# Two-layer graph kernel in fp32: when the scores are masked, squared, scaled and turned, and when the weights' factors are formed

## The chip, the cores and the metric

The kernel runs on one core of one Trainium2 chip. The metric is the device time of the slowest core, here the only one, in microseconds (us), as the median of several runs.

## The reference

64 graphs of 256 nodes and 512 features share one 0/1 adjacency matrix. Two layers are added to the stream x, each behind a layer norm and a relu. What is computed, cut to its core:

```python
h = relu(layernorm(x))                       # layer 0
q, k, v = h @ Wq.T, h @ Wk.T, h @ Wv.T
rel = adj.T * (q @ k.T)                      # scores, masked
rel = rel / norm(rel, axis=2)                # each row to length 1
x = x + rel @ v
h = relu(layernorm(x))                       # layer 1
x = x + (adj @ h) @ weight + bias
```

## The kernel before

The 64 graphs go in 32 pairs. Everything is fp32 and lives in SBUF. Wq and Wk are multiplied once into one matrix M, so that for a pair the work on TensorE is a chain of products: G (h times M), V (h times Wv), the scores (h times G), attend (scores times V, added to x), the gather (adjacency times the second h, called y), and the mix (y times the weight, added to x).

The large products are done by Winograd's form of Strassen's algorithm: seven products of half-size blocks instead of eight. `winograd_steps` (L184) calls them by number, in the order 1, 5, 6, 3, 7, 2, 4, in three PSUM banks: 1, 6, 7 and 4 accumulate one after the other in bank_a. After each product its `take` reads the bank: ScalarE (ACT) copies where the target is new, else VectorE (DVE) adds. `two_levels` (L209) does the same for G, V and the mix, with a second level for two of the products: its steps are called a1, c5, a6, c (a second reading of bank_c), a7, a4, and g1 to g4 (the second-level parts, in bank_d and bank_e). The next product in a bank waits until the last reader of the bank has ended.

The seven products need sums of blocks as operands, and these are DVE work in lists of "steps": `right_operands` (L128, instructions L135 to L138) and `left_factors` (L166, L173 to L176), four instructions each. By use: `gs` for G, `sums` for the transposed h of a later pair, `h_second` and `y_second` for second levels, `y_steps` for the gathered y, `v_steps` and `rel_steps` for the operands of attend (from V and from the turned scores), `w_steps` and `wv_steps` for the weights; `w_second_steps`, `wv_second_steps` and `m_second_steps` for the second level of the weights, once each in the first pairs.

Around the scores (`scores`, L542) there are, for a pair: two masks on DVE (L561, one for each half k of the columns), four squares with row sums on ACT (L566), a root on ACT (L572), an inverse on DVE (L575), four scales on ACT (L578), `place` (L580: 16 transfers on SyncE's queue, which move 32x32 blocks into `placed`), and four 32x32 block transposes on DVE, `turns` (L588, `placed` to `turned`). `turned_i` and `sums_i` (L450, L173 to L176) are the like for the h of pair i; `relus` (L342), `uppers` (L703, ACT) and `lowers` (L707, DVE) form the second h and its split into two parts for exact products at a reduced format; `add_bias` (L719) is four adds on GpSimd (POOL), each possible once ACT has read its quarter of x (the relu).

The order is written out by hand. `run_steps` (L277) calls product after product, and after product n the steps in slot n of a dictionary; TensorE, DVE and ACT keep exactly that order, each in its own queue. In a steady pair (`steady`, L997) the order on TensorE is: attend of pair i interleaved with the rest of V (`attend_and_v`), the scores of pair i+1, G and part of V of pair i+2 (`g_and_v`, L907), the gather of pair i, and the mix of pair i with two parts of G and V (`mix_and_v`, L916). 28 pairs are steady; `first_pairs` (L926) and `last_pairs` (L1045) write out the rest.

The parts of attend by number are `one`, `five`, `six`, `three`, `two`, `seven`, `four` (L672); the mix's g4 follows `one`. `six` reads the operand which `rel_steps[2]` (L175) forms. `norm_by_scalar` (L348) works out the first norm of pair i+4 in the mix: totals and squares on ACT, its root and end.

Of the kernel before, what the change touches and what calls it, by code (L numbers as in the profile page):

```python
# [19 lines left out]
def kernel(  # L20
# [137 lines left out]
    def run(steps):  # L158
        for step in steps:
            step()  # L160
# [112 lines left out]
    def winograd(product, take, side={}, early=False):  # L273

        run_steps(winograd_steps(product, take, early), side)
# [263 lines left out]
        products = v_products(i)  # L539
        return two_levels(*products, *second_weights_moving(HL2[i], wv_second, V[i]))  # L540

    def scores(i, side={}, by_matmul=False):  # L542


        left, right = HL.pop(i), G.pop(i)
        rel = work.tile([P, NB, NC, N], F32, tag="rel", name=f"rel_{i}")
        placed = work.tile([P, NB, NC, NC, P], F32, tag="placed", name=f"placed_{i}")
        turned = work.tile([P, NB, NC, NC, P], F32, tag="turned", name=f"turned_{i}")
        rn = small.tile([P, NB, NC], F32, tag="rn", name="rn")
        R[i] = turned, rel, placed  # L550
# [25 lines left out]

        def scale(b, k):
            nc.scalar.activation(rel[:, b, k], rel[:, b, k], AF.Copy, scale=rn[:, b, k : k + 1])  # L578

        def place():  # L580
            rv = rel.rearrange("p b k (t m) -> p (b k t) m", m=P)
            pv = placed.rearrange("p b k t n -> p (b k t) n")
            for j in range(P // S):
                for k in range(P // S):
                    nc.sync.dma_start(out=pv[ts(j, S), :, ts(k, S)], in_=rv[ts(k, S), :, ts(j, S)])

        def turn(b, k):
            nc.vector.transpose(turned[:, b, :, k], placed[:, b, k])  # L588

        def each(f):  # L590
            return [(lambda b=b, k=k: f(b, k)) for k in range(NC) for b in range(NB)]

        def turn_at_once():
            for b in range(NB):
                pt = ps_m.tile([P, T], F32, tag="pm", name="pr")
                for t in range(NC):
                    for k in range(NC):
                        nc.tensor.transpose(
                            pt[:, ts(t * NC + k, P)], rel[:, b, k, ts(t, P)], ident
                        )  # L600
                nc.scalar.copy(turned[:, b].rearrange("p t k n -> p (t k n)"), pt)

        winograd(product_of_tokens(left, right), take, side)
        if by_matmul:
            masks = [lambda: mask(0), lambda: mask(1)]
            return masks, each(square_sum), root, inverse, rn, turn_at_once
        return (
            [lambda: mask(0), lambda: mask(1)], each(square_sum), root, inverse, each(scale), place,
            each(turn),
        )  # L610

# [102 lines left out]
    def add_bias(i):  # L714

        xt = flat(X[i])
        add = nc.gpsimd.tensor_tensor
        return [
            (lambda c=c: add(xt[:, c, :], xt[:, c, :], bias_bc, ALU.add)) for c in range(TC)  # L719
        ]  # L720
# [205 lines left out]
    def first_pairs(exact):  # L926
# [13 lines left out]
        gs = g_operands(0)  # L940
# [18 lines left out]
        turned2, sums2 = transpose_blocks(2)  # L959
        project_v(1, {  # L960
            0: gs[0:2], 1: gs[2:3] + turned2[0:2], 2: gs[3:4] + turned2[2:4] + relus[0:2],
            3: turned2[4:6] + relus[2:4], 4: turned2[6:8] + m_second_steps[0:4],
            5: m_second_steps[4:8] + turns[0:2], 6: turns[2:4],
        })
        place_blocks(3)
        masks, squares, norm_root, inverse, scales, place, turns = scores(1, {
            0: sums2[0:1], 1: sums2[1:2], 2: sums2[2:3], 3: sums2[3:4], 5: wv_second_steps[0:4],
            6: wv_second_steps[4:8],
        })
        stats, *parts = ln1(0, exact)  # L970
        h_second = second_h.pop(2)()
# [4 lines left out]
        if exact:  # L976
            nc.vector.tensor_copy(adjt_r, adjt_sb)
        g, v = g_and_v(2, by_slot(layer_1(parts), {
            1: h_second + [inverse], 3: scales + [place], 4: turned3[0:1] + add_bias(0), 5: turned3[1:3],
            6: turned3[3:4],  # L980
        }))
        v_steps, rel_steps = attend_operands(1)
        y_steps = gather(0, exact, {
            0: turned3[4:6], 1: turned3[6:8], 2: sums3[0:1], 3: sums3[1:2] + w_second_steps[0:4],
        })
        y_second = second_of_y(0)
        totals, mean, row_squares, *norm0 = norm_by_scalar(flat(X[4]))
        run(y_steps[0:2])
        mixed = mix_and_v(0, g, v, {
            0: y_steps[2:4] + totals[0:2], 1: y_second[0:4] + totals[2:4],  # L990
            2: w_second_steps[4:8] + y_second[4:8] + [mean] + row_squares[0:2],
            3: v_steps[0:2] + row_squares[2:4], 4: turns + rel_steps[0:2] + norm0[0:2],
            5: v_steps[2:4] + sums3[2:4],
        })
        return norm0[2], rel_steps[2:4], mixed, v

    def steady(i, exact, relu0, rel_steps, mixed, v):  # L997

# [5 lines left out]
        stats, root, end, relus, uppers, lowers = ln1(i, exact)  # L1004
        halves = [stats[b * NC + t] for t in range(NC) for b in range(NB)]
        attend_and_v(i, mixed, v, {
            0: rel_steps + relus0[0:2], 1: relus0[2:4] + gs[0:1], 2: gs[1:2],
            3: gs[2:3], 4: gs[3:4] + halves[0:1], 5: halves[1:2],
        })
        if i + 4 < NP:  # L1010
# [3 lines left out]
        h_second = second_h.pop(i + 2)()  # L1014
        masks, squares, norm_root, inverse, scales, place, turns = scores(i + 1, {
            0: halves[2:3], 1: halves[3:4] + h_second[0:1], 2: [root] + h_second[1:4],
            3: [end] + relus[0:1], 4: relus[1:2], 5: uppers[0:1], 6: uppers[1:2],
        })
        turned, sums = transpose_blocks(i + 3)
        bias_steps = add_bias(i)  # L1020
        v_steps, rel_steps = attend_operands(i + 1)
        g, v = g_and_v(i + 2, {
            0: masks + squares[0:2] + lowers[0:1],
            1: squares[2:4] + [norm_root] + lowers[1:2] + turned + [inverse],
            2: relus[2:4],
            3: scales + [place] + sums[0:2],
            4: uppers[2:4] + lowers[2:3] + sums[2:4] + bias_steps,
            5: lowers[3:4] + v_steps[0:2],
        })
        y_products, y_steps = gather_steps(i, exact)  # L1030
        run_steps(y_products, {2: y_steps[0:1]})
        y_second = second_of_y(i)
        totals, row_squares, mean, ends, relu0 = [], [], [], [], None
        if i + 4 < NP:
            totals, step, row_squares, root0, end0, relu0 = norm_by_scalar(flat(X[i + 4]))
            mean, ends = [step], [root0, end0]
        run(y_steps[1:2])
        mixed = mix_and_v(i, g, v, {
            0: y_steps[2:4] + totals[0:2], 1: y_second[0:4] + totals[2:4],
            2: y_second[4:8] + mean + row_squares[0:2],  # L1040
            3: turns + row_squares[2:4], 4: rel_steps[0:2] + ends, 5: v_steps[2:4],
        })
        return relu0, rel_steps[2:4], mixed, v

    def last_pairs(exact, relu0, rel_steps, mixed, v):  # L1045
# [5 lines left out]
        attend_and_v(a, mixed, v, {  # L1051
            0: rel_steps, 1: gs[0:1], 2: gs[1:2], 3: gs[2:3], 4: gs[3:4] + halves[0:1],
            5: halves[1:2],
        })
        h_second = second_h.pop(c)()
        masks, squares, norm_root, inverse, scales, place, turns = scores(b, {
            0: halves[2:3], 1: halves[3:4] + h_second[0:1], 2: [root] + h_second[1:4],
            3: [end] + relus[0:1], 4: relus[1:2], 5: uppers[0:1], 6: uppers[1:2],
        })
        g, v = g_and_v(c, {  # L1060
            0: masks + squares[0:2] + lowers[0:1],
            1: squares[2:4] + [norm_root] + lowers[1:2],
            2: relus[2:4] + [inverse],
            3: scales + [place],
            4: uppers[2:4] + lowers[2:3] + add_bias(a),
            5: lowers[3:4],
        })
        y_steps = gather(a, exact)
# [89 lines left out]
```

## Time and profile before

The median of 3 runs is 1742.64 us (1741.23 to 1745.06). The profiled execution has a span of 1740.6 us at a granted clock of 0.999. One middle pair, from the start of its scores to the start of the next, by stage:

| stage (us from the span's start) | length | PE busy | DVE busy | ACT busy | POOL busy |
|---|---|---|---|---|---|
| scores 887.24 to 893.67 | 6.43 | 6.43 | 5.60 | 2.64 | 0.45 |
| G and V 893.67 to 908.36 | 14.69 | 14.69 | 13.64 | 10.94 | 5.01 |
| gather 908.36 to 912.08 | 3.72 | 3.72 | 2.55 | 1.76 | 0.00 |
| mix 912.08 to 925.57 | 13.49 | 13.49 | 11.59 | 7.21 | 0.00 |
| attend 925.57 to 940.12 | 14.55 | 13.76 | 14.05 | 3.52 | 0.77 |
| sum | 52.88 | 52.09 | 47.43 | 26.07 | 6.22 |

PE is the time in which matmuls are under way, and a matmul held up inside such a stretch doesn't show as idle. A row of a timeline has the start in us, the length in us, the engine, the line, the operation, and output<-inputs; in brackets the idle time of the engine before it and what ended that. Rows of one kind that follow each other are merged (x4). A row of the waits has the total, the number and the longest, in us.

### The profile page before, as it was taken

What the parts mean: (1) busy time and instruction counts of PE and PEld (TensorE: products, weight loads), DVE (VectorE), ACT (ScalarE), POOL (GpSimd) and SP (SyncE); (2) the same over time, 40 slices, a digit from 0 to 9 for tenths busy, and PEclk for the clock granted to TensorE, in tenths of its full rate; (3) what the DMA queues carried; (4) which work ended last, traced back from release to release, by engine and by line L of the source; (5) the groups of instructions that cost most, each with busy time, mean ns of one, the idle gap of its engine ahead of it and who ended that gap; (6) DMA issues with size and microseconds to landing.
All of it is one profiled execution on the core that took longest, in us unless ns stands there. A gap on an engine that the chain in (4) does not pass through costs nothing.

```text
span 1740.6 us, 28453 instructions
## 1 busy us (share of the span) xinstructions
PE 1698.9 (98%) x10274; PEld 1531.7 (88%) x10274; DVE 1523.9 (88%) x3336; ACT 818.3 (47%) x1835; POOL 198.2 (11%) x167
## 2 busy tenths in 40 slices
PE   9999999999999999999999999999999999999997
PEld 7978888898888988888988889988889888889976
DVE  7788989889898889898889898898988898988776
ACT  3444444544445554445544455444455544453331
POOL 0011100111101111001111011110011110011111
PEclk9999999999999999999999999999999999999999
DMA  7413342243332343331343422433323433223101
GB/s 240 63 25 85 75 85 61 38 85 81 78 78 49 57 86 77 82 74 35 74 84 75 86 52 46 85 80 79 79 45 59 86 76 84 69 30 61 34 28 51
DMA packets 425734, 122.56 MB, mean 70 GB/s; under 512 B 398064, under 2 KB 398832, under 8 KB 425584
## 3 DMA queue, kind: packets, MB, share of 16 engines
q1 hardware_dynamic: 412992, 80.28, 25.5%
q0 software_dynamic: 8432, 32.51, 5.3%
q10 hardware_dynamic: 4160, 7.87, 1.3%
q8 instruction: 83, 1.36, 0.3%
q14 instruction: 67, 0.55, 0.1%
HBM read 38.27 MB, written 33.55 MB: 41 GB/s over the span
## 4 chain that ended last, share of the span: by engine, by line
PE 84%; DVE 14%; issue 1%; ACT 0%; DMA 0%; ACTq 0%; DVEq 0%
PE bank_a L299 22%; PE bank_a L287 13%; PE bank_a L311 7%; PE py L735 6%; PE bank_c L299 6%; PE bank_a L658 5%; PE bank_e L525 4%; PE bank_c L287 3%; PE bank_e L478 3%; PE bank_d L525 3%; PE bank_c L311 3%; PE bank_d L478 2%; DVE x_ring L534 2%; PE bank_b L311 2%; DVE x_ring L769 1%; PE bank_b L658 1%
## 5 line engine op out<-in xcount | busy, mean ns | idle before, releaser
L719 POOL TENSOR_TENSOR x_ring<-x_ring,bias_bc 128x512 f32<-128x512 f32 x128 | 173.2, 1374 | 736.5 <-DVE rel L558 443.8
L299 PE MATMUL bank_a<-wv_t,ht 128*128 128x256 f32 x768 | 181.7, 379 | 0.0
L287 PE MATMUL bank_a<-ht,m_t 128*128 128x256 f32 x768 | 181.4, 379 | 0.0
L513 ACT COPY v<-bank_a 128x512 f32<-128x512 f32 x96 | 55.6, 580 | 253.4 <-PE bank_a L299 253.4
L287 PEld LDWEIGHTS bank_a<-ht,m_t 128*128 128x128 f32 x768 | 145.9, 190 | 19.8
L299 PEld LDWEIGHTS bank_a<-wv_t,ht 128*128 128x128 f32 x768 | 143.5, 190 | 18.3
L364 ACT ACTIVATE blocks<-x_ring,sm 128x512 f32<-128x512 f32 x112 | 80.9, 722 | 125.0 <-DVE sm L361 123.2
L735 PE MATMUL py<-adjt_r,h 128*128 128x256 f32 x1024 | 125.9, 280 | 0.1
L342 ACT ACTIVATE h2c<-x_ring,nb,rs 128x512 f32<-128x512 f32 x128 | 97.4, 807 | 56.8 <-DVE nb L339 50.1
L299 PE MATMUL bank_a<-w_t,ys 128*128 128x256 f32 x512 | 121.4, 380 | 0.3 <-DVE x_ring L769 0.3
L735 PEld LDWEIGHTS py<-adjt_r,h 128*128 128x128 f32 x1024 | 120.0, 188 | 0.3 <-DVE h L707 0.3
L790 POOL DMA_DIRECT2D out_dram<-x_ring x31 | 24.1, 776 | 784.9 <-issue 568.1
L739 ACT COPY yt<-py 128x512 f32<-128x512 f32 x128 | 75.0, 587 | 73.2 <-PE py L735 53.8
L299 PEld LDWEIGHTS bank_a<-w_t,ys 128*128 128x128 f32 x512 | 94.9, 190 | 16.0 <-DVE x_ring L769 0.9
L377 ACT ACTIVATE h<-x_ring,nb,rs 128x512 f32<-128x512 f32 x112 | 82.0, 803 | 53.8 <-PE bank_e L525 53.8
L769 DVE TENSOR_TENSOR x_ring<-bank_a,x_ring 128x512 f32<-128x512 f32 x128 | 86.9, 679 | 21.7 <-PE bank_a L299 21.5
L561 DVE TENSOR_TENSOR rel<-rel,adjt_sb 128x512 f32<-128x512 f32 x64 | 68.4, 1106 | 41.3 <-ACT rel L556 41.3
L311 PE MATMUL bank_a<-ht,gt 128*128 128x128 f32 x744 | 101.3, 279 | 0.4 <-DVE rel L558 0.4
L330 DVE BATCH_NORM_STATS2 st<-x_ring 128x6 f32<-128x512 f32 x144 | 97.8, 679 | 0.4
L556 ACT COPY rel<-bank_a 128x256 f32<-128x256 f32 x96 | 35.4, 369 | 129.5 <-PE bank_a L311 58.9
L311 PEld LDWEIGHTS bank_a<-ht,gt 128*128 128x128 f32 x744 | 90.4, 192 | 3.6 <-DVE rel L558 0.6
L665 DVE TENSOR_TENSOR x_ring<-bank_a,x_ring 128x512 f32<-128x512 f32 x116 | 78.8, 679 | 10.7 <-PE bank_a L658 10.7
(221 smaller groups left out, 4084.7 us busy)
## 6 DMA issues: line engine op xcount, KB each, us to landing
blocks<-h SPq DMA_DIRECT2D x496, 64.0 KB, 3.6
out_dram<-x_ring POOLq DMA_DIRECT2D x31, 1024.0 KB, 5.4
x_ring<-in_x_dram SPq DMA_DIRECT2D x28, 1024.0 KB, 6.1
placed<-rel SPq DMA_DIRECT2D x496, 32.0 KB, 2.0
x_ring<-in_x_dram ACTq DMA_DIRECT2D x4, 1024.0 KB, 5.4
wq_sb<-in_L_gnn_Wq_dram SPq DMA_DIRECT2D x4, 256.0 KB, 4.7
wk_sb<-in_L_gnn_Wk_dram ACTq DMA_DIRECT2D x4, 256.0 KB, 6.0
wv_sb<-in_L_gnn_Wv_dram ACTq DMA_DIRECT2D x1, 1024.0 KB, 5.5
```

The source lines that it names most:

```text
L287: nc.tensor.matmul(bank[:, e * HT_ : (e + 1) * HT_], right[n][:, d, ts(e, P)], left[n][:, d, :], start=(start and e == 0 and d == 0), stop ...
L299: nc.tensor.matmul(bank[:, b * HD : (b + 1) * HD], left[n][:, d, ts(b, P)], right[n][:, d, :], start=(start and b == 0 and d == 0), stop=( ...
L311: nc.tensor.matmul(bank[:, ts(b, P)], right[n][:, d, ts(b, P)], left[n][:, d, ts(b, P)], start=(start and b == 0 and d == 0), stop=(d == H ...
L330: nc.vector.bn_stats(st[:, c, :], src[:, c, :])
L342: nc.scalar.activation(dst, src[:, c, :], AF.Relu, bias=nb[:, c : c + 1], scale=rs[:, c : c + 1])
L377: nc.scalar.activation(dst, src[:, c, :], AF.Relu, bias=nb[:, c : c + 1], scale=rs[:, c : c + 1])
L478: nc.tensor.matmul(out, m_second[k][n], HL2[i][k][n], start=start, stop=True, skip_group_check=True)
L525: nc.tensor.matmul(out, left[k][n], right[k][n], start=start, stop=True, skip_group_check=True)
L658: nc.tensor.matmul(bank[:, ts(b, HD)], left[n][:, b], right[n][:, b], start=(start and b == 0), stop=True, skip_group_check=True,)
L719: (lambda c=c: add(xt[:, c, :], xt[:, c, :], bias_bc, ALU.add)) for c in range(TC)
L735: nc.tensor.matmul(pm[:, d, :], left[:, b * NC + m, ts(d0 + d, P)], right, start=(n == 0), stop=(n == len(terms) - 1),)
L769: nc.vector.tensor_add(xt[block], bank.rearrange("p (b e) -> p b e", b=NB), xt[block])
```

## The change

Four things move; no instruction on TensorE is added, removed or reordered.

- In `scores` with `inside=True`, the mask and the squares of the half k = 1 of the columns, which is complete after the fifth product, go into slots 5 and 6 of the scores. The other half, the root, the inverse, the scales and `place` go into slot 0 of G, ahead of the uppers, which leave the scores.
- `turns` go from slot 3 of the mix to the end of the gather, ahead of `y_steps[1]`.
- All four `rel_steps` then run in slots 3 and 4 of the mix; before, the last two ran in slot 0 of attend.
- In the first pairs the second-level factors of the weights, and the transposes and sums of pair 3, are dealt out differently; in the last mix but one `y_second[4:8]` comes a slot earlier, and the lowers a slot later.

What it is for: operands of attend are to be ready before attend begins.

```diff
-    def scores(i, side={}, by_matmul=False):
+    def scores(i, side={}, by_matmul=False, inside=False):
...
+        masks, squares = [lambda: mask(0), lambda: mask(1)], each(square_sum)
+        if inside:
+            side = by_slot(side, {5: masks[1:], 6: squares[2:]})
+            masks, squares = masks[:1], squares[:2]
         winograd(product_of_tokens(left, right), take, side)
...
     # first_pairs
         project_v(1, {
-            3: turned2[4:6] + relus[2:4], 4: turned2[6:8] + m_second_steps[0:4],
+            3: turned2[4:6] + relus[2:4] + w_second_steps[0:4],
+            4: turned2[6:8] + m_second_steps[0:4],
...
         masks, squares, norm_root, inverse, scales, place, turns = scores(1, {
-            0: sums2[0:1], 1: sums2[1:2], 2: sums2[2:3], 3: sums2[3:4], 5: wv_second_steps[0:4],
-            6: wv_second_steps[4:8],
+            0: sums2[0:1], 1: sums2[1:2], 2: sums2[2:3], 3: sums2[3:4], 5: w_second_steps[4:8],
...
         g, v = g_and_v(2, by_slot(layer_1(parts), {
-            1: h_second + [inverse], 3: scales + [place], 4: turned3[0:1] + add_bias(0), 5: turned3[1:3],
-            6: turned3[3:4],
+            1: h_second + [inverse], 2: turned3[0:4], 3: scales + [place] + turned3[4:8],
+            4: add_bias(0) + wv_second_steps[0:4], 5: sums3[0:2], 6: wv_second_steps[4:8],
         }))
-        y_steps = gather(0, exact, {
-            0: turned3[4:6], 1: turned3[6:8], 2: sums3[0:1], 3: sums3[1:2] + w_second_steps[0:4],
+        y_products, y_steps = gather_steps(0, exact)
+        run_steps(y_products, {
+            0: sums3[2:3], 1: sums3[3:4], 2: y_steps[0:1], 3: v_steps[0:1],
         })
-        run(y_steps[0:2])
+        run(y_steps[1:2])
         mixed = mix_and_v(0, g, v, {
             0: y_steps[2:4] + totals[0:2], 1: y_second[0:4] + totals[2:4],
-            2: w_second_steps[4:8] + y_second[4:8] + [mean] + row_squares[0:2],
-            3: v_steps[0:2] + row_squares[2:4], 4: turns + rel_steps[0:2] + norm0[0:2],
-            5: v_steps[2:4] + sums3[2:4],
+            2: y_second[4:8] + [mean] + row_squares[0:2], 3: v_steps[1:2] + row_squares[2:4],
+            4: turns + rel_steps[0:2] + norm0[0:2], 5: rel_steps[2:4] + v_steps[2:4],
         })
     # steady
         attend_and_v(i, mixed, v, {
-            0: rel_steps + relus0[0:2], 1: relus0[2:4] + gs[0:1], 2: gs[1:2],
+            0: relus0[0:2], 1: relus0[2:4] + gs[0:1], 2: gs[1:2],
...
         masks, squares, norm_root, inverse, scales, place, turns = scores(i + 1, {
-            3: [end] + relus[0:1], 4: relus[1:2], 5: uppers[0:1], 6: uppers[1:2],
-        })
+            3: [end] + relus[0:1], 4: relus[1:2],
+        }, inside=True)
         g, v = g_and_v(i + 2, {
-            0: masks + squares[0:2] + lowers[0:1],
-            1: squares[2:4] + [norm_root] + lowers[1:2] + turned + [inverse],
+            0: masks + squares + [norm_root] + turned[0:4] + [inverse] + scales + [place],
+            1: uppers[0:2] + turned[4:8] + lowers[0:2],
             2: relus[2:4],
-            3: scales + [place] + sums[0:2],
-            4: uppers[2:4] + lowers[2:3] + sums[2:4] + bias_steps,
+            3: uppers[2:4] + sums[0:2],
+            4: lowers[2:3] + sums[2:4] + add_bias(i),
             5: lowers[3:4] + v_steps[0:2],
         })
-        run_steps(y_products, {2: y_steps[0:1]})
+        run_steps(y_products, {2: y_steps[0:1], 3: turns})
         run(y_steps[1:2])
         mixed = mix_and_v(i, g, v, {
             2: y_second[4:8] + mean + row_squares[0:2],
-            3: turns + row_squares[2:4], 4: rel_steps[0:2] + ends, 5: v_steps[2:4],
+            3: rel_steps[0:2] + row_squares[2:4], 4: root0 + rel_steps[2:4] + end0,
+            5: v_steps[2:4],
         })
     # last_pairs: scores(b) with inside=True, and
         g, v = g_and_v(c, {
-            0: masks + squares[0:2] + lowers[0:1],
-            1: squares[2:4] + [norm_root] + lowers[1:2],
-            2: relus[2:4] + [inverse],
-            3: scales + [place],
-            4: uppers[2:4] + lowers[2:3] + add_bias(a),
+            0: masks + squares + [norm_root, inverse] + scales + [place],
+            1: uppers[0:2] + lowers[0:2],
+            2: relus[2:4],
+            3: uppers[2:4],
+            4: lowers[2:3] + add_bias(a),
...
     # mix of the last pair but one
-            0: y_second[0:4] + [root], 1: [end] + relus[0:2] + uppers[0:2],
-            2: y_second[4:8] + lowers[0:1] + relus[2:3], 3: lowers[1:2] + relus[3:4],
-            4: uppers[2:4] + add_bias(c), 6: lowers[2:3], 7: lowers[3:4],
+            0: y_second[0:4] + [root], 1: y_second[4:8] + [end] + relus[0:2] + uppers[0:2],
+            3: lowers[0:1] + relus[2:3], 4: lowers[1:2] + relus[3:4],
+            5: uppers[2:4] + add_bias(c), 6: lowers[2:3], 7: lowers[3:4],
```

More of the change, by code (lines that the diff above doesn't have):

```diff
@@ L601, in turn_at_once @@
                 nc.scalar.copy(turned[:, b].rearrange("p t k n -> p (t k n)"), pt)
+        masks, squares = [lambda: mask(0), lambda: mask(1)], each(square_sum)
+        if inside:
+            side = by_slot(side, {5: masks[1:], 6: squares[2:]})
+            masks, squares = masks[:1], squares[:2]
         winograd(product_of_tokens(left, right), take, side)
         if by_matmul:
-            masks = [lambda: mask(0), lambda: mask(1)]
-            return masks, each(square_sum), root, inverse, rn, turn_at_once
+            return masks, squares, root, inverse, rn, turn_at_once
         return (
-            [lambda: mask(0), lambda: mask(1)], each(square_sum), root, inverse, each(scale), place,
+            masks, squares, root, inverse, each(scale), place,
             each(turn),
@@ L987, in first_pairs, with steady @@
         totals, mean, row_squares, *norm0 = norm_by_scalar(flat(X[4]))
-        run(y_steps[0:2])
+        run(y_steps[1:2])
         mixed = mix_and_v(0, g, v, {
             0: y_steps[2:4] + totals[0:2], 1: y_second[0:4] + totals[2:4],
-            2: w_second_steps[4:8] + y_second[4:8] + [mean] + row_squares[0:2],
-            3: v_steps[0:2] + row_squares[2:4], 4: turns + rel_steps[0:2] + norm0[0:2],
-            5: v_steps[2:4] + sums3[2:4],
-        })
-        return norm0[2], rel_steps[2:4], mixed, v
-    def steady(i, exact, relu0, rel_steps, mixed, v):
+            2: y_second[4:8] + [mean] + row_squares[0:2], 3: v_steps[1:2] + row_squares[2:4],
+            4: turns + rel_steps[0:2] + norm0[0:2], 5: rel_steps[2:4] + v_steps[2:4],
+        })
+        return norm0[2], mixed, v
+    def steady(i, exact, relu0, mixed, v):
         gs = g_operands(i + 1)
@@ L1016, in steady @@
             0: halves[2:3], 1: halves[3:4] + h_second[0:1], 2: [root] + h_second[1:4],
-            3: [end] + relus[0:1], 4: relus[1:2], 5: uppers[0:1], 6: uppers[1:2],
-        })
+            3: [end] + relus[0:1], 4: relus[1:2],
+        }, inside=True)
         turned, sums = transpose_blocks(i + 3)
-        bias_steps = add_bias(i)
         v_steps, rel_steps = attend_operands(i + 1)
         g, v = g_and_v(i + 2, {
-            0: masks + squares[0:2] + lowers[0:1],
-            1: squares[2:4] + [norm_root] + lowers[1:2] + turned + [inverse],
+            0: masks + squares + [norm_root] + turned[0:4] + [inverse] + scales + [place],
+            1: uppers[0:2] + turned[4:8] + lowers[0:2],
             2: relus[2:4],
-            3: scales + [place] + sums[0:2],
-            4: uppers[2:4] + lowers[2:3] + sums[2:4] + bias_steps,
+            3: uppers[2:4] + sums[0:2],
+            4: lowers[2:3] + sums[2:4] + add_bias(i),
             5: lowers[3:4] + v_steps[0:2],
@@ L1030, in steady @@
         y_products, y_steps = gather_steps(i, exact)
-        run_steps(y_products, {2: y_steps[0:1]})
+        run_steps(y_products, {2: y_steps[0:1], 3: turns})
         y_second = second_of_y(i)
-        totals, row_squares, mean, ends, relu0 = [], [], [], [], None
+        totals, row_squares, mean, root0, end0, relu0 = [], [], [], [], [], None
         if i + 4 < NP:
-            totals, step, row_squares, root0, end0, relu0 = norm_by_scalar(flat(X[i + 4]))
-            mean, ends = [step], [root0, end0]
+            totals, *middle, relu0 = norm_by_scalar(flat(X[i + 4]))
+            mean, row_squares, root0, end0 = [middle[0]], middle[1], [middle[2]], [middle[3]]
         run(y_steps[1:2])
@@ L1040, in steady, with last_pairs @@
             2: y_second[4:8] + mean + row_squares[0:2],
-            3: turns + row_squares[2:4], 4: rel_steps[0:2] + ends, 5: v_steps[2:4],
-        })
-        return relu0, rel_steps[2:4], mixed, v
-    def last_pairs(exact, relu0, rel_steps, mixed, v):
+            3: rel_steps[0:2] + row_squares[2:4], 4: root0 + rel_steps[2:4] + end0,
+            5: v_steps[2:4],
+        })
+        return relu0, mixed, v
+    def last_pairs(exact, relu0, mixed, v):
         a, b, c = NP - 3, NP - 2, NP - 1
@@ L1051, in last_pairs @@
         attend_and_v(a, mixed, v, {
-            0: rel_steps, 1: gs[0:1], 2: gs[1:2], 3: gs[2:3], 4: gs[3:4] + halves[0:1],
-            5: halves[1:2],
+            1: gs[0:1], 2: gs[1:2], 3: gs[2:3], 4: gs[3:4] + halves[0:1], 5: halves[1:2],
         })
@@ L1057, in last_pairs @@
             0: halves[2:3], 1: halves[3:4] + h_second[0:1], 2: [root] + h_second[1:4],
-            3: [end] + relus[0:1], 4: relus[1:2], 5: uppers[0:1], 6: uppers[1:2],
-        })
+            3: [end] + relus[0:1], 4: relus[1:2],
+        }, inside=True)
         g, v = g_and_v(c, {
-            0: masks + squares[0:2] + lowers[0:1],
-            1: squares[2:4] + [norm_root] + lowers[1:2],
-            2: relus[2:4] + [inverse],
-            3: scales + [place],
-            4: uppers[2:4] + lowers[2:3] + add_bias(a),
+            0: masks + squares + [norm_root, inverse] + scales + [place],
[3 more added lines that the diff above has]
+            4: lowers[2:3] + add_bias(a),
             5: lowers[3:4],
```

## The prediction

> **What bounds the kernel now.** I read the page's busy times and chain first, then the waits of TensorE, then one middle pair as a timeline, engine by engine.
>
> ```profile
> PE 1698.9 (98%) x10274; PEld 1531.7 (88%) x10274; DVE 1523.9 (88%) x3336; ACT 818.3 (47%) x1835; POOL 198.2 (11%) x167
> ...
> PE 84%; DVE 14%; issue 1%; ACT 0%; DMA 0%; ACTq 0%; DVEq 0%
> ```
> TensorE (PE) sets the time. No matmul is added or removed, so only its idle time can change: 1740.6 - 1698.9 = 41.7 us. The waits of PE, largest two:
>
> ```profile
> PE bank_a L658 <- DVE rel L175: 21.8, 29, 2.0
> PE bank_e L525 <- DVE x_ring L534: 3.9, 2, 2.4
> ```
> The first is 27 x 0.72, one of 2.05 and one of 0.35. It is PE in the timeline of one pair (period 52.88 us):
>
> ```profile
> 901.47 1.89 PE L287 MATMUL bank_a<-ht,m_t 128*128 128x256 f32 x8
> ...
> 905.82 1.89 PE L287 MATMUL bank_a<-ht,m_t 128*128 128x256 f32 x8
> ...
> 925.57 1.03 PE L658 MATMUL bank_a<-v,turned 128*128 128x256 f32 x4
> 926.67 0.49 PE L525 MATMUL bank_e<-w_t,yt 128*128 128x128 f32 x2
> ...
> 929.86 1.13 PE L658 MATMUL bank_a<-placed,rel 128*128 128x256 f32 x4 [0.72 <-DVE rel L175]
> ```
> The last row is `six` of attend. Undisturbed spacings are 0.87 for four L658 rows, 0.55 for g4, 0.89 for v's g1, so from 925.57 it could start at 925.57 + 0.87 + 0.55 + 0.87 + 0.89 = 928.75. It starts 1.11 later. Besides the listed 0.72, g4 starts at 926.67 instead of 926.44, right behind the add that empties its bank; this wait has no row of its own. VectorE (DVE) in the same pair, and GpSimd:
>
> ```profile
> 901.35 0.90 DVE L173 TENSOR_TENSOR ht<-ht 128x512 f32<-128x512 f32 x1
> 902.28 1.65 DVE L174 TENSOR_TENSOR ht<-ht 128x512 f32<-128x512 f32 x1
> 903.85 0.68 DVE L466 TENSOR_TENSOR g<-bank_c,g 128x512 f32<-128x512 f32 x1
> 904.45 0.68 DVE L466 TENSOR_TENSOR g<-bank_a,g 128x512 f32<-128x512 f32 x1
> ...
> 926.20 0.41 DVE L534 TENSOR_TENSOR x_ring<-bank_e,x_ring 128x256 f32<-128x256 f32 x1
> ...
> 929.39 0.41 DVE L175 TENSOR_TENSOR rel<-turned 128x256 f32<-128x256 f32 x1
> ```
> ```profile
> 900.43 2.95 POOL L719 TENSOR_TENSOR x_ring<-x_ring,bias_bc 128x512 f32<-128x512 f32 x2 [4.71 <-ACT h2c L342]
> ```
> L173 and L174 take 0.68 and 0.69 elsewhere; here 0.90 and 1.65, under the two bias adds. The add at 904.45 empties bank_a for a4 of G (PE at 905.82): it ends at 905.13, 0.69 early.
>
> **What the Trainium skill says.** "GPSIMD Engine Reference", section 8 (Key points): GpSimd shares its SBUF interfaces with VectorE and contends with DVE instructions of two SBUF inputs or of a 2-port mode. The trace agrees and shows that it is all or nothing: L174 starts at 902.28 while GpSimd's second add runs to 903.38 and ends 0.55 after it; GpSimd's second add (901.65) lasts 1.73 instead of 1.27, since L173 held it up. They alternate. Adds with a PSUM source aren't slowed (L466 at 104.13 under a bias add: 0.69). "PSUM — Partial Sum Buffer", section "PSUM bank collisions raise a hardware error", wants banks guarded by semaphores: hence a product that accumulates in a bank waits for the bank's last reader, the wait of g4 above.
>
> **The change, part by part.** Times are on the clock of this pair.
>
> 1. Turns and rel_steps, steady pairs. Nothing is added; in the mix the four transposes (920.79, 1.41) make room for rel_steps[0:2] (0.80), and rel_steps[2:4] (0.88) go to slot 4, out of attend. DVE then: a4's add of the mix 925.24, L534 ends 926.25 (before 926.61), so g4 keeps 926.44. v_steps[2:4] (0.72 + 0.60) still follow, then `one`'s add, 928.09 to 928.77; `six` uses the same bank and starts at 928.83 instead of 929.86. Gain 1.03.
>
> 2. Turns after gather's last product. DVE is idle there (0.84 before L173 at 911.09, 1.12 before L174 at 912.90). L173 is followed by four transposes at 0.33 each: L174 starts at 913.03 instead of 912.90, ends 913.72, and c5 of the mix needs it at 913.81. Priced at 0.03 a pair, 0.14 if it just misses. The transfer behind the turns takes 10.4 us of issue (903.88 on) and 2.0 to landing; it now starts at 899.2 (below), lands at 911.3, before the turns at 911.7. Nothing.
>
> 3. Masks and squares in the scores. mask(1) can start behind bank_b's add, 892.80 + 0.33 = 893.13; the first bias add starts at 893.22. DVE goes first; GpSimd's add then ends at 894.95, mask(0) (ready 894.28) at 894.95 + 0.53 = 895.48. ScalarE (ACT): a4's copy at 893.88, squares k=1, G's a1 copy at 895.60 (PE's time, as before), squares k=0 from 896.08, root ends 0.94 + 0.20 later, 897.22; inverse to 897.40; scales from 897.45. DVE's transposes (turned[0:4], 895.4 to 896.8) have one input and should not stand behind GpSimd.
>
> 4. What the scales push back. They now precede everything else on ACT: 1.60 for four, so G's c5 copy is at 899.05 (before 897.33; nobody needs it sooner), the first upper U = 899.53, a6's copy U + 1.05 to U + 1.64 = 901.17. PE's a7 needs that copy at 901.47: 0.3 spare. relu2 follows at U + 1.53 (before 899.54, now 901.06), and the third bias add 0.89 after it, U + 2.42 = 901.95 (before 900.43).
>
> 5. What this meets. DVE: lower0 at U + 0.65, lower1 at U + 1.25, G's two g1 adds at U + 1.85 and U + 2.18, sums0 (L173) at U + 2.51. The bias add is 0.09 ahead. By item 3's pattern it goes first: ends U + 3.69; L173 ends 0.55 later, U + 4.24; the fourth bias add takes its turn, to U + 5.37; L174 ends 0.55 later, U + 5.91. Then c's add, then a7's add from U + 6.43 to U + 7.11 = 906.64. a4 of G needs it at 905.82 and starts at 906.70: a new wait of 0.88, with the restart (spacing 0.97 instead of 0.87 after a wait) 0.97. Queued behind on DVE: g2's add, two lowers, sums, v_steps, g3's adds; they shift along with PE, so nothing further is lost.
>
> 6. First pairs. Now 1.04 + 1.37 + 1.53 + 2.05 us are waited (c5 of the mix, w's second factors, g4, six). In the new order turned3 (8 x 0.33) and wv's factors (8 x 0.3) stand among the adds of G and V. DVE has done lower1 at 103.4, turned3 fills it to 106.1, a7's add ends at 107.4, and a4 of G, ready at 106.55, waits 0.9. Then lower2, wv's first four, lower3, two sums, g3's adds, wv's last four: 113.5; two sums, y_steps[0], v_steps[0]: L174 from 116.0 to 116.7, c5 at 116.75 (ready 115.4) waits 1.3, though w's factors no longer follow it. In the mix DVE then stays 1 us behind: turns end at 128.4, rel and norm0 at 129.6, L534 at 130.6: g4 waits 1.3; v_steps and `one`'s add end at 133.9: six starts at 133.95 instead of 136.28. Gain 2.3.
>
> 7. Last pairs. The 0.35 wait goes (0.45 with the restart). In the last mix but one the second factors of y (8 instructions, 1.1) now stand in front of a6's add, which ends at 1706.96 instead of 1706.09: a7 starts at 1707.0 instead of 1706.14. But lower0 no longer stands in front of g1's adds: these end at 1708.2, and g2 follows a7 at 1708.8 instead of 1710.55. lower0 to lower3 come one slot later, each behind a bias add at worst; the last ends near 1715.0, and the gather that needs it resumes there instead of at 1718.5 (lower3's end before). Gain 3.4.
>
> Sum: -27 x 1.03 = -27.8; +28 x 0.97 = +27.2; +28 x 0.03 = +0.8; -2.3 - 0.45 - 3.4. Together -6.0: 1742.6 - 6.0 = 1736.6, say 1737. The wait removed is nearly all paid back by the new one.
>
> **The rivals.** A: DVE gets SBUF first in item 5. For it: the lead is only 0.09 on chains of six spacings. Against: each spacing is read to 0.02. Then a7's add ends at U + 6.07 = 905.60 and a4 does not wait: 1737 - 27 = 1710. B, slower than before: the scales come late, because GpSimd wins at mask(1) (it starts 0.09 later, so hardly) or because transposes do stand behind its adds (the only ones overlapping now, near 900.5, are not slowed: longest L450 is 0.445). Scales then start 0.67 later, a6's copy ends at 901.84, a7 waits 0.5 with restart, a4 again 0.97: 28 x 0.5 = 14 more, 1751. C: A and B together, 1737 - 27 + 14 = 1724.
>
> **How the numbers follow.** Likeliest 0.68; A 0.13; B 0.13; C 0.06. The likeliest is itself uncertain by some 5 us (c5 up to 0.14 x 28 = 4, items 6 and 7 by 2 each), so of it 0.65 lie below 1739.2 (faster by 0.2%), 0.30 within, 0.05 above 1746.1. Faster 0.44 + 0.13 + 0.06 = 0.63; same 0.20; slower 0.04 + 0.13 = 0.17. The range 1711 to 1750 leaves out about half of A and half of B and the outermost of the rest.
>
> **What would show it.** L175's wait at L658 gone in middle pairs (item 1). A wait of PE L287 (a4) for DVE L466 of about 0.9 in 28 pairs (item 5); none of it means A. L173 of the sums lasting about 1.7 and L174 1.65. Third bias add near 901.95 on this clock. A wait of a7 for ACT's L464 copy means B; waits of c5 for L174, item 2. If stream transposes last over 0.5 under bias adds, item 3 is wrong.

## The result, and the profile after

The changed kernel takes 1766.63 us (median of 4 runs, 1762.73 to 1768.10), the kernel before beside it 1741.93 (1740.59 to 1745.06): ratio 1.0136, 95% interval 1.0114 to 1.0157. The change makes the kernel 1.4% slower. The prediction said 1737.0 with a range of 1711 to 1750: wrong in direction, and outside its range.

The profiled span is 1764.8 us, 24.2 longer than before (1740.6). From the page of the kernel after, busy times and the chain that ended last (line numbers from L543 on are 1 to 4 higher than before):

```profile
PE 1707.8 (97%) x10274; PEld 1530.4 (87%) x10274; DVE 1535.3 (87%) x3336; ACT 812.3 (46%) x1835; POOL 225.2 (13%) x167
...
PE 41%; DVE 17%; issue 17%; SPq 14%; DMA 7%; ACT 4%; DVEq 0%; POOLq 0%; ACTq 0%
```
Each engine has the same number of instructions as before, but the chain is another. Before it was 84% PE; now PE holds 41%, and SyncE's queue (SPq), "issue" and DMA, which had 1% together, hold 38%. The waits of TensorE, largest two:

```profile
PE bank_a L287 <- DVE g L466: 24.1, 28, 0.9
PE bank_a L287 <- ACT g L464: 15.2, 21, 2.0
```
L175's wait is gone, as meant. The first row is a4 of G behind the sums, the new wait that the prediction named, in 28 pairs. The second is a7 of G behind ACT's copy of a6; the likeliest forecast did not have it, its rival B did. The waits of DVE tell where it starts:

```profile
DVE ht L450 <- DMA blocks<-h: 36.4, 26, 2.8
```
Before, that row was `1.0, 1, 1.0`: the block transposes of h (`turned`) now stand waiting for their transfers. Before, in the pair of the table, all eight stood behind the lowers and followed them without a wait:

```profile
898.00 2.72 DVE L450 STREAM_TRANSPOSE ht<-blocks 128x256 f32<-128x256 f32 x8
```
One middle pair of the kernel after in the timeline, its scores starting at 842.76, DVE first:

```profile
849.79 1.23 DVE L562 TENSOR_TENSOR rel<-rel,adjt_sb 128x512 f32<-128x512 f32 x1 [0.45 <-ACT rel L557]
852.79 1.43 DVE L450 STREAM_TRANSPOSE ht<-blocks 128x256 f32<-128x256 f32 x4 [1.77 <-DMA blocks<-h]
854.14 0.14 DVE L576 RECIPROCAL rn<-rn 128x4 f32<-128x4 f32 x1
...
858.91 1.71 DVE L173 TENSOR_TENSOR ht<-ht 128x512 f32<-128x512 f32 x1
860.65 1.65 DVE L174 TENSOR_TENSOR ht<-ht 128x512 f32<-128x512 f32 x1
...
862.82 0.67 DVE L466 TENSOR_TENSOR g<-bank_a,g 128x512 f32<-128x512 f32 x1
```
ACT in the same pair, the scales and the copy of a6:

```profile
854.31 1.71 ACT L579 ACTIVATE rel<-rel,rn 128x256 f32<-128x256 f32 x4 [1.57 <-DVE rn L576]
...
857.42 0.58 ACT L464 COPY g<-bank_a 128x512 f32<-128x512 f32 x1
```
PE, a7 and a4 of G:

```profile
858.06 1.99 PE L287 MATMUL bank_a<-ht,m_t 128*128 128x256 f32 x8 [0.91 <-ACT g L464]
...
863.55 1.99 PE L287 MATMUL bank_a<-ht,m_t 128*128 128x256 f32 x8 [0.88 <-DVE g L466]
```
Read in order: DVE is through the mask at 851.02 and stands for 1.77 until the transfers have landed; the inverse is queued behind the transposes, though its root on ACT ended at 852.74; ACT stands 1.57 for the inverse, then scales, copies c5, splits two uppers and only then copies a6, to 858.00; PE starts a7 at 858.06. Why the transfers are late stands in SyncE's queue, after and before (start, and the length of the issuing; the rows around the start of one scores):

```profile
833.48 2.90 SPq L440 DMA_DIRECT2D blocks<-h  x3
838.82 0.38 SPq L90 DMA_DIRECT2D x_ring<-in_x_dram  x1
839.24 11.87 SPq L440 DMA_DIRECT2D blocks<-h  x13
```
```profile
877.27 4.92 SPq L440 DMA_DIRECT2D blocks<-h  x4
882.65 0.37 SPq L90 DMA_DIRECT2D x_ring<-in_x_dram  x1
883.06 10.63 SPq L440 DMA_DIRECT2D blocks<-h  x12
```
On this queue the load of x for pair i+4 stands among the 16 block transfers of pair i+3, and it waits for the output transfer that frees its slot of x. After, it stands one place earlier: three transfers are issued, the queue stands from 836.38 to 838.82 (2.44 us), and 13 are still to come; before, it stood 0.46 (882.19 to 882.65), with 12 to come. In both kernels the load is issued 5.3 to 5.4 us after the first block transfer; what differs is how many transfers are out by then. In the source the load is called ahead of all 16, before and after, so its place in the queue is settled when the program is built; why the change moved it by one, no run shows. Over the whole kernel this wait of SyncE for the output went from 15.8 us to 64.4:

```profile
SPq L90 <- DMA out_dram<-x_ring: 64.4, 27, 3.7
```
The last transfer is issued 6.45 us after the start of the scores before (893.69 - 887.24), and 8.35 after it now (851.11 - 842.76). The pair shown is a late one: in the median of 28 pairs it is 6.57 before and 7.92 after.

Where the 24.2 us come from, by the mean distance from start to start of the products on TensorE, over 28 periods of steady pairs (each term with the restart: the product that follows a waited one comes 0.10 to 0.15 later):

| us per pair, against before | forecast | after |
|---|---|---|
| attend (g4 and six) | -1.03 | -1.02 |
| a4 of G | +0.97 | +1.09 |
| a7 of G | 0 | +0.83 |
| gather and c5 of the mix | +0.03 | +0.09 |
| period | -0.03 | +1.00 |

28 x 0.996 = +27.9; the first pairs give -0.5, the last -3.2: +24.2.

### The profile page after: what moved, and what is told of

The parts are those of the page before. It is cut to its first block, busy times and chain, and to the rows that moved or that the text cites. A ratio compares the mean times of both kernels' runs of the same rounds, so it can differ in the third digit from the quotient of the medians.

```text
span 1764.8 us, 28451 instructions
## 1 busy us (share of the span) xinstructions
PE 1707.8 (97%) x10274; PEld 1530.4 (87%) x10274; DVE 1535.3 (87%) x3336; ACT 812.3 (46%) x1835; POOL 225.2 (13%) x167
## 4 chain that ended last, share of the span: by engine, by line
PE 41%; DVE 17%; issue 17%; SPq 14%; DMA 7%; ACT 4%; DVEq 0%; POOLq 0%; ACTq 0%
PE bank_a L299 14%; SPq L440 13%; PE py L739 5%; PE bank_a L287 4%; DMA out_dram<-x_ring 4%; DMA blocks<-h 3%; PE bank_e L525 3%; PE bank_c L299 3%; DVE ht L173 3%; PE bank_a L662 2%; ACT rel L579 2%; DVE ht L174 2%; PE bank_d L525 2%; DVE ht L450 2%; DVE h L711 2%
## 5 line engine op out<-in xcount | busy, mean ns | idle before, releaser
L723 POOL TENSOR_TENSOR x_ring<-x_ring,bias_bc 128x512 f32<-128x512 f32 x128 | 200.3, 1585 | 759.2 <-DVE rel L559 424.6
L287 PE MATMUL bank_a<-ht,m_t 128*128 128x256 f32 x768 | 188.5, 389 | 39.4 <-DVE g L466 24.1
L287 PEld LDWEIGHTS bank_a<-ht,m_t 128*128 128x128 f32 x768 | 142.3, 191 | 77.9 <-DVE g L466 35.3
L711 DVE TENSOR_TENSOR h<-h2c,h 128x512 fp32r<-128x512 f32 x128 | 86.7, 698 | 43.4 <-ACT h L707 43.4
L450 DVE STREAM_TRANSPOSE ht<-blocks 128x256 f32<-128x256 f32 x248 | 86.7, 409 | 39.2 <-DMA blocks<-h 36.4
L773 DVE TENSOR_TENSOR x_ring<-bank_a,x_ring 128x512 f32<-128x512 f32 x128 | 88.0, 687 | 23.7 <-PE bank_a L299 23.6
L464 ACT COPY g<-bank_a 128x512 f32<-128x512 f32 x96 | 56.0, 584 | 87.4 <-PE bank_a L287 87.4
```

The source lines that it names most:

```text
L287: nc.tensor.matmul(bank[:, e * HT_ : (e + 1) * HT_], right[n][:, d, ts(e, P)], left[n][:, d, :], start=(start and e == 0 and d == 0), stop ...
L450: nc.vector.transpose(ht[:, d, half].rearrange("p (b n) -> p b n", b=NB), by_half[:, :, half, d])
L711: nc.vector.tensor_sub(dst[:, 1, c, :], whole_h[c], dst[:, 0, c, :].bitcast(F32))
L773: nc.vector.tensor_add(xt[block], bank.rearrange("p (b e) -> p b e", b=NB), xt[block])
```

## Experiments

The theory after the result: the first four transposes, moved ahead of the inverse and asked for earlier, meet transfers that come later; everything behind them on DVE and ACT slips until a7 of G is late. The main rival: the scales are simply too much for ACT at this place (the prediction's "0.3 spare" never existed), and DVE's wait is a bystander. Terms per pair below are measured as in the table above. Each ratio is to the kernel before as it ran beside that run: its median was 1743.08 us for e1 to e4, 1745.78 for e5 to e8 and 1744.75 for e9, so runs of different groups are compared by ratio or by term, not by time.

**e1: the inverse ahead of the transposes.**

```diff
-            0: masks + squares + [norm_root] + turned[0:4] + [inverse] + scales + [place],
+            0: masks + squares + [norm_root, inverse] + scales + [place] + turned[0:4],
```


> The changed kernel with one step moved: in slot 0 of G the inverse, the scales and the placing stand ahead of turned[0:4] on VectorE's queue instead of behind it. Theory T (a7's wait comes from the scales being late because the inverse queues behind transposes that wait for the block transfers): a7's waits of 15.2 us for ACT's copy go, the 28 waits of a4 for DVE stay at 0.9, time about 1740 (1766 - 26). Rival S (the four scales in front of a6's copy on ACT are too long in themselves): a7's waits stay, time 1760 to 1768.

1742.05 us, ratio 0.9992 (0.9986 to 0.9999) to the kernel before. a7's term is 0.00, a4's 1.02, attend's -1.02. ACT has the same work in the same order ahead of a6's copy, and a7 isn't late: the rival falls. The scales have room, if the inverse doesn't stand behind the transfers.

**e2: the load of x behind all 16 block transfers.** Nothing on DVE, ACT or PE is reordered.

```diff
+        place_blocks(i + 3)
         if i + 4 < NP:
             load(i + 4)
-        place_blocks(i + 3)
```


> The changed kernel with the load of a later x queued on SyncE behind the 16 block transfers instead of between the third and the fourth. Theory T, with the load's own wait for the output transfer as what makes the blocks late: DVE's 36 us of waits for blocks go, a7's waits with them, time about 1740. Rival Q (the blocks are late only because attend got shorter by 1 us): they come some 0.6 to 1 us earlier at most, a7's waits fall by half, time 1750 to 1758. Rival S: time unchanged, 1766.

1740.54 us, ratio 0.9981 (0.9973 to 0.9990). SyncE, DVE and GpSimd in the timeline of e2, around scores that start at 834.08:

```profile
824.80 13.81 SPq L440 DMA_DIRECT2D blocks<-h  x16
838.77 0.51 SPq L90 DMA_DIRECT2D x_ring<-in_x_dram  x1
```
```profile
842.27 1.41 DVE L450 STREAM_TRANSPOSE ht<-blocks 128x256 f32<-128x256 f32 x4
844.10 0.18 DVE L576 RECIPROCAL rn<-rn 128x4 f32<-128x4 f32 x1 [0.42 <-ACT rn L573]
```
```profile
840.06 3.42 POOL L723 TENSOR_TENSOR x_ring<-x_ring,bias_bc 128x512 f32<-128x512 f32 x2 [14.65 <-DVE rel L559]
```
The last transfer is issued 4.53 us after the scores start, DVE's wait for the transfers is gone, and so is a7's term (0.00). The inverse now waits only for its root. With the transfers in time the kernel is what the prediction described: attend -1.02, a4 +0.99, c5 +0.10. It also shows the part of item 3 that could not be seen before: the four transposes take 1.41 us, most of it under a bias add, no more than elsewhere. e1 and e2 take away the same wait of a7 at two ends, by order on DVE and by order on SyncE. From the first block transfer to the end of issuing the last it is 13.32 us in e2 and 17.20 after (medians of 28 pairs). The stand of the queue for the load, 2.46 after, is most of the difference; that the load of 1 MB moves beside the transfers after, and behind them in e2, may have a part in the rest, which no run separates.

**e6: the load behind the fourth transfer, where the kernel before has it.**

```diff
     def place_blocks(i, between=None):
...
+            if j == 1 and between: between()
...
-        if i + 4 < NP:
-            load(i + 4)
-        place_blocks(i + 3)
+        place_blocks(i + 3, (lambda: load(i + 4)) if i + 4 < NP else None)
```


> The changed kernel with the load on SyncE behind the fourth block transfer, where the kernel before has it, instead of behind the third. If the queue's order and the shorter attend share the lateness (0.6 and 1.0 us of some 1.5): DVE's 36 us of waits for blocks about halve, a7's waits too, time 1748 to 1755. If the order alone does it: no such waits, 1740. If attend's length alone: 1764 to 1768.

1753.46 us, ratio 1.0047 (1.0030 to 1.0064). a7's term falls from 0.83 to 0.36, not to 0. So, taken away first, the one place in SyncE's queue is more than half of it; the rest has another cause.

**e7: the mix and attend as before.** Only the part of the change in the scores and in G is kept; the turns are back in slot 3 of the mix and the last two `rel_steps` in attend.

```diff
-            0: relus0[0:2], 1: relus0[2:4] + gs[0:1], 2: gs[1:2],
+            0: late.pop(i, []) + relus0[0:2], 1: relus0[2:4] + gs[0:1], 2: gs[1:2],
...
-        run_steps(y_products, {2: y_steps[0:1], 3: turns})
+        run_steps(y_products, {2: y_steps[0:1]})
...
-            3: rel_steps[0:2] + row_squares[2:4], 4: root0 + rel_steps[2:4] + end0,
+            3: turns + row_squares[2:4], 4: rel_steps[0:2] + root0 + end0,
...
+        late[i + 1] = rel_steps[2:4]
...
```


> Only the scores and G part of the change, in steady pairs: the turns, and where rel_steps run, are as in the kernel before, so that attend waits as before (27 waits of 0.7 for L175); the load comes behind the fourth transfer here too. If the blocks are late only against a shorter attend: DVE's waits for blocks under 4 us, no waits of a7, a4's waits of 0.7 to 0.9 in all 28 pairs, time 1742 + 28 x 0.9 - 5 = about 1762 to 1766. If the early masks themselves make the transposes ask too soon: waits for blocks of 20 us or more stay, time 1780 or more.

1771.58 us, ratio 1.0145 (1.0128 to 1.0162), between the two forecasts; DVE's waits for blocks are 7.8 us, which lies between them too. The waits of PE in e7:

```profile
PE bank_a L287 <- DVE g L466: 22.3, 29, 0.9
PE bank_a L662 <- DVE rel L175: 19.7, 28, 0.7
PE bank_a L287 <- ACT g L464: 2.2, 3, 1.2
```
a7's wait is nearly gone (3 pairs, term 0.15), though the transposes stand ahead of the inverse as in the kernel after; attend's wait is back beside a4's. In this kernel the load stands behind the fourth transfer again, though nothing in its edit moves it. So e6 and e7 separate the two causes: the load's place takes a7's term from 0.83 to 0.36, attend's length from 0.36 to 0.15. The link is visible: from the first block transfer to the start of the scores it is 9.97 us before and 9.96 in e7, but 9.28 after and 9.27 in e6 (means of 27 pairs, each within 0.02). Transfers start with the first norm of pair i+3, in attend; a shorter attend brings the scores, and what they ask for, 0.69 us nearer to them. That the change gains in attend is itself part of why it loses in G.

What is left in e7 has neither cause: there the last transfer is issued as before (6.56 us after the scores start, before 6.57), and only the transposes ask sooner. The start of the first transposes shows the three parts directly. In the median it is 8.19 us after the start of the scores in e2, where nothing is late, 8.40 in e7, 9.01 in e6 and 9.55 after: 0.21 from asking sooner, 0.61 from the shorter attend, 0.54 from the load's place. On PE the shares are others, since a7 has some slack that is used up first, and they depend on which part is taken away first.

**e3: without the late bias adds.** The third and fourth bias add of steady pairs are left out, so half of the rows lack their bias.

```diff
-            4: lowers[2:3] + sums[2:4] + add_bias(i),
+            4: lowers[2:3] + sums[2:4] + add_bias(i)[0:2],
```


> The changed kernel without the third and fourth bias add of each steady pair (half of the rows go without the bias there). Theory P (a4's wait of 0.88 is the sums' L173 and L174 standing behind these two adds at the shared SBUF interface): L173 and L174 take 0.68, the 28 waits of a4 go, time about 1766 - 27 = 1739. Rival D (VectorE simply has too much ahead of a7's add): a4 keeps at least half of its wait, time 1752 or more.

1742.22 us, ratio 0.9989 (0.9980 to 0.9998). a4's term goes from 1.09 to 0.00; a7's stays at 0.78. The meeting of sums and bias adds is the whole of a4's wait, and a7's hardly depends on it. c5 now costs 0.36; e4 below has the reason.

**e5: the sums one slot later**, so that they follow the bias adds; all bias adds are kept.

```diff
-            3: uppers[2:4] + sums[0:2],
-            4: lowers[2:3] + sums[2:4] + add_bias(i),
+            3: uppers[2:4],
+            4: lowers[2:3] + sums[0:4] + add_bias(i),
```


> The changed kernel with only sums[0:2] behind a7's add of G. Theory P with T: the 28 waits of a4 go (27 us) and a7's waits of 15 us for ACT stay, time about 1739 to 1742; with e1 (1742) and e4 (1719) the two causes then add up. Rival: if a7's lateness alone makes a4 late, a4 keeps waits and the time stays over 1750.

1740.03 us, ratio 0.9970 (0.9958 to 0.9982): a4 0.00, a7 0.91, c5 0.24.

**e4: e1 and e5 together; e8: e1, e2 and e5 together.**

> e1's edit and, besides, sums[0:2] behind a7's add of G instead of ahead of it. Theories T and P: both new waits go, the gain in attend of 1.03 us a pair stays, time 1709 to 1716, faster than both kernels. Rivals: if the bias adds now hold up the lowers or y_steps, the gather or c5 waits instead, time 1725 to 1742.

> Inverse first, sums[0:2] later, load behind all block transfers. After e4 (1718.7) no wait for blocks is left on the path, so the load's place should add nothing: 1717 to 1720. If late blocks still cost something in e4 (c5's waits of 5 us for yt), it gives up to 5 us more: 1713.

e4 takes 1718.65 us, ratio 0.9853 (0.9837 to 0.9870); e8 1718.65 us, ratio 0.9844 (0.9827 to 0.9860). Both are faster than the kernel before and the kernel after, though e4 misses its forecast of 1709 to 1716. a7 and a4 are at 0.00, attend at -1.01 to -1.02, but gather and c5 are at 0.30, 8 us over 28 pairs, where the kernel after has 0.09. The waits of DVE and of PE in e4:

```profile
DVE turned L589 <- DMA placed<-rel: 4.7, 8, 1.1
PE bank_c L299 <- DVE yt L174: 5.4, 9, 1.1
```
That is the same oversight a second time, in small: `turns`, moved to the end of the gather, wait for the transfers of `place`, and L174 behind them makes c5 late. The kernel after, e1 and e2 have no such wait; e3, e4, e5 and e8, in which the gather starts sooner because a4 no longer waits, have it 7 to 11 times each. DVE in e4, after the transposes of a middle pair:

```profile
789.14 0.69 DVE L466 TENSOR_TENSOR g<-bank_a,g 128x512 f32<-128x512 f32 x1 [0.44 <-PE bank_a L287]
...
790.69 0.68 DVE L173 TENSOR_TENSOR ht<-ht 128x512 f32<-128x512 f32 x1
791.40 0.69 DVE L174 TENSOR_TENSOR ht<-ht 128x512 f32<-128x512 f32 x1
```
The sums last 0.68 and 0.69 instead of 1.71 and 1.65, since GpSimd ended at 790.22 (787.70 + 2.52, not shown), and the add that empties bank_a for a4 now waits for PE instead of the other way round. e8 adds nothing to e4: with the inverse first, it no longer matters to PE when the block transfers of h land.

**e9: rel_steps alone.** The kernel before with one edit, attend's two `rel_steps` moved into the mix, and no turns moved to make room.

```diff
-            3: turns + row_squares[2:4], 4: rel_steps[0:2] + ends, 5: v_steps[2:4],
+            3: turns + row_squares[2:4], 4: rel_steps[0:2] + ends[0:1] + rel_steps[2:4] + ends[1:2],
+            5: v_steps[2:4],
         })
-        return relu0, rel_steps[2:4], mixed, v
+        return relu0, [], mixed, v
```


> The kernel before, with one edit: rel_steps[2:4] go from attend's slot 0 to the mix's slot 4; turns, scores, G and the first and last pairs stay as before. If making room (turns out of the mix, so the scales earlier in G) is what makes the shorter attend possible: in the pair shown, the adds that empty bank_e for g4 end 0.5 to 0.8 later, since 0.79 of DVE work now stands ahead of them and only 0.27 of idle time is there to take it; g4 starts at 927.2 to 927.5 instead of 926.67, six at 929.5 to 929.8 instead of 929.86: 0.1 to 0.4 a pair, 1732 to 1741 us beside 1743 of before. If the place of rel_steps alone gives the whole 1.03 a pair, near 1715. If the earlier scores run into the block transfers here too, slower than before, with new waits of DVE L450 for the transfers.

1740.48 us, ratio 0.9972 (0.9959 to 0.9986). The largest wait of PE in e9:

```profile
PE bank_e L525 <- DVE x_ring L534: 19.2, 30, 2.4
```
L175's wait became g4's, 0.56 in a middle pair, and attend's term is -0.17 where the full change has -1.02. So the room that the turns leave in the mix is needed for the gain in attend; moving the operands alone shifts DVE's work by a slot and the wait with it. That the turns can leave only if the scales come earlier was not run; it follows from the timeline before, where `place` is issued until 914.26 and the gather has ended at 912.08.

## Why the prediction was wrong

- **Item 1 (attend): right.** Forecast -1.03, measured -1.02; e9, without the room that the turns leave, has -0.17.
- **Item 2 (c5): right that it is small.** Forecast +0.03, measured +0.09. Of it c5's own start has 0.015 and the product behind it 0.05; 0.02 lie in the gather ahead of it. Its "Nothing" for the transfers behind the turns held in the kernel after, with little to spare: once a4 is on time, the turns wait for them (e4).
- **Item 3: the step that failed.** Its times up to there hold: mask(0) ends 8.26 us after the start of the scores (forecast 895.48, which is 8.24), the root 9.98 (forecast 897.22, also 9.98). Then it said "DVE's transposes (turned[0:4], 895.4 to 896.8) have one input and should not stand behind GpSimd". The item asked which engine might hold DVE up, and answered that rightly (e2). It put at nothing what the transposes themselves wait for, the block transfers on SyncE's queue. Measured, that wait is 1.77 us in the pair shown and 36.4 us in 26 waits of the whole kernel, and the inverse and the scales stand behind it. In the pair shown of before the block transfers were issued to 893.69, and the transposes came at 898.00 in a full DVE, so nothing waited and no row pointed there. The landing takes some 1.7 (852.79 - 851.11 after), which puts it near 895.4, an estimate: the change asks for the transposes 2.5 us sooner (895.4 to 895.5, against 898.00), just when the transfers of before had landed. There was nothing left for a delay; e7 shows that this alone costs 0.15 a pair.
- **The delay itself was overlooked.** The order on SyncE's queue is three transfers, the load, thirteen (in 26 of 27 pairs), where before it is four and twelve; the prediction read the orders of DVE and ACT and not that of this queue. And item 1's own gain moves the scores toward the transfers; the item counted only what PE gains. Together the last issue comes 1.9 us later after the start of the scores in the pairs shown (8.35 against 6.45), of which 1.2 lie on the queue and 0.7 in the shorter attend; in the median it is 1.35. e6 and e7 show both parts.
- **Item 4: right in its chain, wrong in its start.** "0.3 spare" for a7 becomes a lateness: the scales start 11.55 after the start of the scores instead of 10.21, 1.34 later, and a6's copy ends 1.31 later than forecast (15.24 against 13.93). PE needs it at 14.23 (901.47 - 887.24) and starts a7 at 15.30: 1.07 late in this pair. In the median the scales start at 11.07, and at 10.23 in e1 and e2, as forecast. Over 28 pairs a7 costs 0.83 a pair, or 23 us. The forecast was 1737, the kernel takes 1766.6: this is most of the difference.
- **Item 5: right.** The third bias add starts 0.11 ahead of L173 (forecast 0.09), L173 takes 1.71 (1.73), L174 1.65, and a4 waits 0.88 in this pair. With a7 on time a4 starts 19.47 after the start of the scores, in e1 and in e2; the forecast was 906.70 - 887.24 = 19.46. The term is 0.99 in e2 (forecast 0.97), and 1.09 after. So rival A, DVE first, was rightly not taken.
- **Item 6: too large.** The first steady scores start at 146.00 instead of 146.54. Counted from the first scores of all, it is 95.3 us in the kernel after, e1, e2 and e6, which have the same first pairs, and 96.4 before: a gain of 1.1 instead of 2.3 (the profiled execution after began 0.5 later). The item priced only what comes from G on: w's second factors now stand among the scores of pair 1, whose last product waits 1.08 for DVE's L559 instead of 0.41.
- **Item 7: right.** From the last steady scores to the last mix it is 90.39 us instead of 93.57: 3.2 gained, forecast 0.45 + 3.4.
- **The rivals.** B had the right chain, scales late, a6's copy late, a7 waits, and even the right side (slower than before); it gave two reasons for late scales, GpSimd's win at the mask and slowed transposes, and the runs show neither. The true one was a third. So the size was off (0.5 a pair, measured 0.83), and that its time of 1751 lies nearer to the result than 1737 was luck. Its chance of 0.13 weighed the two reasons that had been found, not the fact that "0.3 spare" was all that stood between the forecast and B.

With the transfers in time (e2) the measured effect is -0.2%, near the forecast's -0.3%. The sum nearly holds for a kernel whose block transfers land in time. It does not for one that only keeps the load's old place (e6, +0.5%).

## What to carry to other kernels

When a step moves earlier, list everything that it waits for, transfers included, with its slack in the old order; a wait that no row shows may have been hidden by the very delay that is taken away. Compare the order of the issuing queue too, and ask what a transfer at its head waits for. A short step on the critical chain (here an inverse of 0.14 us) does not belong behind work that depends on a transfer.

## What the runs showed of the hardware

A transfer that waits at the head of SyncE's queue holds all that stands behind it: in the pair shown, 13 transfers for 2.44 us, where before 12 were held for 0.46. The Trainium skill, page "DMA: Bandwidth & Descriptors", section "Anatomy of one DMA — SWDGE (gpsimd) path", says that the DMA engines never wait on semaphores and that the issuing sequencer does, before dispatch. The trace agrees: SyncE's queue itself has the wait for the output, 64.4 us in 27 times, and with the waiting load put last (e2) the 16 block transfers are issued without a break in 13.81 us. The DMA engines were not idle meanwhile: in the 2.44 us their mean busy share was 0.92, against some 0.3 over the whole kernel.

The contention of GpSimd with DVE instructions of two SBUF inputs, which the page "GPSIMD Engine Reference" states in section 8 (Key points), is a matter of 2 us a pair here: two sums took 3.4 us under two bias adds and 1.4 us behind them (e4), while four transposes with one input took 1.41 us, most of it under a bias add (e2). Its form is alternation, instruction by instruction: in the pair shown GpSimd's adds end at 860.07 and 861.75, and L173 and L174 each 0.55 later, at 860.62 and 862.30.
